# The second sequence's mLSTM cell moved ahead of all attention, four heads to a step

## The chip, the cores and the metric

The kernel runs on one core of one Trainium2 chip. The metric is device time in microseconds of one launch. A core has five engines that each work through their own queue: TensorE (PE, matrix products; PEld is its weight loads), VectorE (DVE), ScalarE (ACT), GpSimd (POOL) and SyncE (SP, which only issues transfers). Transfers are also issued by ACT and POOL. Lines such as L421 are lines of the kernel before.

## The reference, cut to what matters

Eight sequences of 512 tokens and 256 features go through four stages, each added to the running value:

```
x = x + tanh(g_xattn[0]) * mlstm_cell(layernorm(x), ctx, ctx)   # 8 heads of 32
x = x + tanh(g_ffn[0])   * attention32_and_experts(layernorm(x))  # 32 heads of 8, then 8 experts
x = x + tanh(g_xattn[1]) * cross_attention(ctx, layernorm(x))   # 16 heads of 16
x = x + tanh(g_ffn[1])   * product_key_memory(layernorm(x))     # 4096 rows
```

The change concerns the first stage alone. For each head the cell computes

```
log_f = log_sigmoid(fg);  cs = cumsum(log_f)
log_D = cs[:, None] - cs[None, :] + ig[None, :]     # lower triangle, else -inf
D     = exp(log_D - max(log_D))
C     = (q @ k.T) / sqrt(32) * D
h     = (C / (max(|sum(C)|, exp(-max)) + eps)) @ v
```

and then normalises h over the features. Here q is the normalised x, and k and v are the context.

## The kernel before, in words

**Stages.** `attention_phase` does the first three stages of all eight sequences (m = 0 to 7). The memory (the fourth stage) follows and isn't touched.

**What sets the order.** Inside `attention_phase` the order of TensorE's instructions is the order in which Python emits them. All other engines are ordered by a scheduler that weighs the whole program. The emitting loop goes through 24 attention jobs of 16 steps: ("A", m, f), half f of the 32 heads, and ("C", m, 0), the cross attention. A step has a first pass for one job, which finds the maxima (`maxima`: scores at L421, then the row maximum on DVE at L439), and a second pass for an earlier job (`exponentials`: scores at L421 again, exp on ACT at L468; then `values`, L484). Both go in two half steps. At the start there are steps in which nothing of attention is ready, then 19 steps with a first pass alone, and from then on mostly both.

Beside the steps, `beside` fills TensorE's queue from eight *lanes*, generators that are asked in order of priority. A lane yields a cost (it has emitted that much TensorE work), ("wait", t) (come back later by the plan's clock), ("rest", key) (come back when the key is in `rested`), or ("take", flag) for the one PSUM bank that cells and experts share. The lanes are: `between` (loads each job's operands into SBUF and marks it ready), `values1`, `after`, `before` for sequences 0, 2, 3, ... 7 with the class `Tiles`, `behind` (experts and the cross attention's queries), `before` for sequence 1 with the class `Lent`, `contexts` (the cross attention's keys and values), and `fill` (first-layer products of the memory, the filler).

**A cell.** `before` calls `cell(m, own, loaded)` and then `queries(m, own, Xa)`, which makes q, k and v of the 32 heads and stores them to DRAM. In `cell`: layer norm of x (statistics L98, normalise L107), transposes to features (L350), the gates (`gp`, L736), a chain on ACT and DVE for the running sums and maxima (L745 to L774), the maxima out to DRAM (`nM_d`, L776) and back to all partitions. Then per pair of heads and per block c of 128 keys: a triangular mask on POOL, the decay exp on ACT, scores on PE, their product with the decay on DVE, and sums on PE. `close` transposes the sums (L804) and divides.

There are two forms of that middle part. `all_pairs`, used for sequence 0 alone, has eight steps of two pairs (four heads) each; it reads all four maxima tiles at once, into the `qa`/`ka` tiles of set 1 that attention doesn't use yet (L644), keeps decays in set 2 and in attention's `pr` tiles, and scores in attention's `sc` banks and sums in its `av` bank. It is emitted in one piece. Sequences 1 to 7 use the loop over pairs, which has one maxima tile (two for `Lent`) and small banks of its own, and yields after each block (L829 fetch, L847 mask, L855 decay, L877 scores, L882 product, L862 sums).

`Lent` holds the second cell's tiles in places of the expert weights, which are free at the start. Its x and context are loaded by SP (L579, L622, L582), those of other sequences by POOL behind `settled`, the last piece of sequence 0's v. `Tiles.begin` of the third sequence also spreads its context into `cte` on POOL (L227).

Of the kernel before, what the change touches and what calls it, by code (L numbers as in the profile page):

```python
# [21 lines left out]
P = 128  # L22
# [14 lines left out]
def kernel(  # L37
# [27 lines left out]
    nc = tc.nc  # L65
# [114 lines left out]
    def attention_phase(ctx: ExitStack):  # L180
# [86 lines left out]
        for w, src in ((wo2, w0[3]), (wq3, w3[0])):  # L267
# [20 lines left out]
        sets = [  # L288
            tuple(cst.tile([P, 4, S], F32, name=f"{name}{i}") for name in ("qa", "ka"))
            for i in range(3)  # L290
        ]
# [270 lines left out]
        class Tiles:  # L562
# [23 lines left out]
            def context(self, m):  # L586
                return load_context(m, "cTc"), cte

            ahead = False

            def maximum(self, n=0):
                return cel.tile([P, 2, S], F32, name="mb", bufs=1)

            def pair(self):
# [8 lines left out]
        class Lent(Tiles):  # L603
# [18 lines left out]
                self.loader.dma_start(cT, cxT[order[m]].rearrange("(k p) s -> p k s", p=P))  # L622
                return cT, self.cte

            ahead = True

            def maximum(self, n=0):
                return self.more[:, n % 2].rearrange("p c d -> p (c d)").rearrange(
                    "p (i s) -> p i s", i=2
                )  # L630

            def pair(self):
                self.n += 1
# [2 lines left out]
            def stream(self):  # L636
                return self.more[:, 1]

        def all_pairs(qT, cT, ce, nM_d, aT, close):


            room = [t[:, 2 * i : 2 * i + 2] for t in sets[1] for i in range(2)]
            for pair in range(4):
                nc.sync.dma_start(  # L644
                    room[pair], nM_d[2 * pair : 2 * pair + 2].partition_broadcast(P)
                )
            spare = [t[:, 2 * i : 2 * i + 2] for t in sets[2] for i in range(2)]
            pds, avs = {}, {}
            steps = [(g, c) for g in range(2) for c in range(NC)]

            def decay(n):
                g, c = steps[n]
                s0 = c * P
                for pair in (2 * g, 2 * g + 1):
                    mb = room[pair]

                    nc.gpsimd.affine_select(
                        out=mb[:, :, s0 : s0 + P], in_=mb[:, :, s0 : s0 + P],
                        pattern=[[0, 2], [1, P]], compare_op=ALU.is_ge,
                        fill=NEG, base=0, channel_multiplier=-1,  # L660
                    )
                    pd = pds[pair, c] = (
                        spare[c - 1 + pair % 2] if c % 2
                        else prb.tile([P, 2, S], F32, name="pr", tag="pr")
                    )
                    for i in range(2):
                        h = 2 * pair + i
                        nc.scalar.activation(
                            pd[:, i, s0:], mb[:, i, s0:], AF.Exp, bias=aT[:, c, h : h + 1]
                        )  # L670

            def weigh(n):
                g, c = steps[n]
                s0 = c * P
                two = {
                    pair: ps_sc.tile([P, 2, S], F32, name="sc", tag="sc")
                    for pair in (2 * g, 2 * g + 1)
                }
                for pair, sc in two.items():
                    for i in range(2):  # L680
                        r = 32 * (2 * (pair % 2) + i)
                        nc.tensor.matmul(
                            sc[:, i, s0:], cT[r : r + 32, g, s0 : s0 + P], qT[r : r + 32, g, s0:],
                            start=True, stop=True,
                        )
                for pair, sc in two.items():
                    pd = pds[pair, c]
                    nc.vector.scalar_tensor_tensor(
                        pd[:, :, s0:], sc[:, :, s0:], 1.0 / math.sqrt(32.0), pd[:, :, s0:],
                        ALU.mult, ALU.mult,  # L690
                    )

            def sums(n):
                g, c = steps[n]
                for pair in (2 * g, 2 * g + 1):
                    if c == 0:
                        avs[pair] = (
                            ps_av.tile([P, S], F32, name="av", tag="av") if pair % 2
                            else ps_ac.tile([P, S], F32, name="cav", tag="ac")
                        )  # L700
                    for i in range(2):
                        h = 2 * pair + i
                        nc.tensor.matmul(
                            avs[pair][64 * i : 64 * i + 64, c * P :],
                            ce[:, c, 33 * h : 33 * h + 64],
                            pds[pair, c][:, i, c * P :], start=(c == 0), stop=(c == NC - 1),
                        )

            decay(0)
            decay(1)  # L710
            for n in range(len(steps) + 1):
                if n < len(steps):
                    weigh(n)
                if n > 0:
                    sums(n - 1)
                    g, c = steps[n - 1]
                    if c == NC - 1:
                        for pair in (2 * g, 2 * g + 1):
                            close(pair, avs[pair])
                if n + 2 < len(steps):  # L720
                    decay(n + 2)

        def cell(m, own, loaded):
            b = order[m]
            qn, cT, ce = loaded or own.begin(m)
            yield ("wait", 4)
            yield from layernorm(qn, qn, "q" + own.user)
            qT = own.features("qT")
# [46 lines left out]
            nM_d = drm.tile([8, S], F32, name="nM_d")  # L775
# [9 lines left out]
            aT = small.tile([P, NC, 8], F32, name="aT")  # L785
# [9 lines left out]
            def store_sums(av):  # L795
                avs = trp.tile([P, S], F32, name="avs", tag="pk", bufs=2)
                nc.any.tensor_copy(avs, av)
                return avs
# [21 lines left out]
                    ALU.mult,  # L820
                )

            if m == 0:
                all_pairs(qT, cT, ce, nM_d, aT, lambda pair, av: close(pair, store_sums(av)))
            mbs = {}

            def fetch_maximum(pair):
                mbs[pair] = own.maximum(pair)
                nc.sync.dma_start(  # L829
                    mbs[pair], nM_d[2 * pair : 2 * pair + 2].partition_broadcast(P)  # L830
                )

            for pair in range(4) if m else ():

                if pair not in mbs:
                    fetch_maximum(pair)
                    yield ("wait", 2.5)
                mb = mbs[pair]
                if own.ahead and pair < 3:
                    fetch_maximum(pair + 1)  # L840
                g = pair // 2
                pds = {}

# [27 lines left out]
                av = own.bank("cav")  # L871
# [24 lines left out]
                yield ("wait", 1.0)  # L896
                close(pair, avs)
                yield 0.7
                if pair == 2:
                    rested.add(("cell", m))  # L900
            Xa = own.stream()
            with behind_first():
                nc.gpsimd.dma_start(Xa, x[b].rearrange("(c p) d -> p c d", p=P))
# [87 lines left out]
        def begin(m):  # L991
            for f in range(2):
                i, last = block2_set(m, f)
                yield ("rest", ("q", m))
                if last is None and i:
                    prepare(i)
                if last:
                    yield ("rest", last)
                for half, src, name in zip(sets[i], qks[m], "qk"):
                    yield ("rest", (name, m))  # L1000
                    spread(half, src, 32 * f, 8)
                    if name == "q":
                        blank(half)
                yield ("wait", LANDING)
                ready.add(("A", m, f))
                yield ("rest", ("v_d", m))
                yield ("rest", ("A", m - 1, f))
                nc.sync.dma_start(v0[f][:, :, : 16 * 9], vds[m][:, f])
                ready.add(("v0", m, f))
# [271 lines left out]
        ready, rested = set(), set()  # L1281

        def before(sequences, tiles):
            own, loaded = tiles(), None
            if tiles is Lent:
                loaded = own.begin(sequences[0])
                yield ("rest", ("k", 0))
            for m in sequences:
                if m == 2:
                    yield ("rest", ("cell", 1))  # L1290
                Xa = yield from cell(m, own, loaded)
                yield from queries(m, own, Xa)
            if tiles is Lent:
                rested.add(("lent", 0))
                load_first(0)
                load_second(0)
# [239 lines left out]
    def close(p, h):  # L1536

        nc.tensor.matmul(
            scores[p, h], ones3, crow[:, 512 * h : 512 * h + 512], start=False, stop=True
        )  # L1540
# [115 lines left out]
    pieces = activations()  # L1656
# [192 lines left out]
    ahead = weights_of(*steps[0])  # L1849
# [3 lines left out]
    for g, (p, u) in enumerate(steps):  # L1853
        n, step = g // 8, g % 8
        q = p + 2
        cf, ahead = ahead, weights_of(*steps[g + 1]) if g + 1 < len(steps) else None
# [100 lines left out]
```

## Time and profile before

| | us |
|---|---|
| median of 3 runs | 3799.53 (3795.38 to 3808.29) |
| the profiled execution | 3788.9 |
| its span | 3787.1 |
| first attention score (L421) | 100.86 |
| first step with both passes | 234 |
| PE busy in the span | 3495.5 (92%) |

In the profile each engine has a busy time; a row of the timeline gives the start, the time that a group of instructions took, the engine, line and operation, what it wrote and read, and in brackets the idle time of that engine before it and what ended it. A windows row gives the stretch, its length, the busy time of the engines in the order PE, PEld, DVE, ACT, POOL with the number of instructions, the granted TensorE clock, the DMA share and GB/s.

### The profile page before, as it was taken

The numbers are of one execution on the slowest core, as the hardware profiler recorded it, in microseconds if no ns is written. First come the engines' busy times: TensorE is split into PE (matmuls) and PEld (weight loads), VectorE is DVE, ScalarE is ACT, GpSimd is POOL, SyncE is SP. The second block draws the span as 40 slices with busy tenths as digits, with TensorE's granted clock in tenths as the row PEclk, the third lists the DMA queues.
The fourth block names the chain that finished last, engine by engine and source line by source line (L and its number), as shares of the span: only waits on it lengthen the run. The fifth ranks groups of instructions, "written<-read, shape, count | busy, mean of one in ns | idle before, by whom it ended". The sixth has DMA issues, their size and how long they took to land.

```text
span 3787.1 us, 76231 instructions
## 1 busy us (share of the span) xinstructions
PE 3495.5 (92%) x31049; PEld 1827.5 (48%) x31049; DVE 2244.9 (59%) x5490; ACT 1755.2 (46%) x2300; POOL 601.5 (16%) x646
## 2 busy tenths in 40 slices
PE   5789888998999999999999999999899999999998
PEld 2333333443443444344433444434346777777776
DVE  4565655665555555555555553544422789999993
ACT  2135444453444445444555444444442455555551
POOL 3121102111100110101100110100000133333331
PEclk7789999999999999999999999999999999999999
DMA  3422212322412332323231232320434433333331
GB/s 112 127 83 82 69 44 71 92 75 65 125 51 78 92 90 77 94 82 98 83 90 57 92 102 81 104 88 23 146 119 144 127 116 106 105 105 106 107 106 38
DMA packets 225195, 345.35 MB, mean 91 GB/s; under 512 B 25982, under 2 KB 173470, under 8 KB 216542
## 3 DMA queue, kind: packets, MB, share of 16 engines
q1 hardware_dynamic: 206796, 277.43, 24.5%
q0 software_dynamic: 16864, 62.46, 5.6%
q8 instruction: 244, 4.00, 0.4%
q14 instruction: 107, 0.88, 0.1%
q10 hardware_dynamic: 1184, 0.58, 0.1%
HBM read 238.50 MB, written 101.09 MB: 90 GB/s over the span
## 4 chain that ended last, share of the span: by engine, by line
PE 66%; DVE 7%; ACT 2%; DMA 1%; issue 1%; SPq 0%; DVEq 0%; ACTq 0%
PE sc L421 16%; PE acc L1799 12%; PE ps_hd L131 11%; PE av L484 6%; DVE nm L439 5%; PE cf L1779 4%; PE ps_sim L1531 3%; PE ps_y L1063 2%; PE ps_h L1044 2%; PE ps_q L380 2%; PE ps_p L369 1%; PE ps_hl L131 1%; PE cav L862 1%; PE csc L877 1%; PE ps_g L1180 1%
## 5 line engine op out<-in xcount | busy, mean ns | idle before, releaser
L439 DVE TENSOR_REDUCE nm<-sc 128x2 f32<-128x1024 f32 x768 | 939.0, 1225 | 926.2 <-PE sc L421 924.2
L468 ACT ACTIVATE pr<-sc 128x1024 f32<-128x1024 f32 x768 | 782.8, 1023 | 928.9 <-PE sc L421 928.4
L421 PE MATMUL sc<-ka,qa 32*128 32x512 f32 x3072 | 906.2, 652 | 96.9 <-DVE nm L439 96.0
L421 PE MATMUL sc<-qa,ka 32*128 32x512 f32 x3072 | 858.3, 647 | 29.1 <-ACT pr L468 27.3
L1799 PE MATMUL acc<-up_sb,gs 64*128 64x256 f32 x4096 | 467.9, 381 | 1.3 <-DVE gs L1788 1.3
L421 PEld LDWEIGHTS sc<-ka,qa 32*128 32x128 f32 x3072 | 246.3, 186 | 437.4 <-DVE nm L439 248.6
L131 PE MATMUL ps_hd<-xT,dw 128*64 128x256 f32 x3584 | 431.2, 385 | 20.7 <-DMA dw<-in_down 9.5
L484 PE MATMUL av<-pr,v 128*32 128x512 f32 x3072 | 414.3, 611 | 3.0 <-DMA v<-v_d 2.9
L1799 PEld LDWEIGHTS acc<-up_sb,gs 64*128 64x128 f32 x4096 | 389.6, 187 | 52.4 <-issue 4.9
L131 PEld LDWEIGHTS ps_hd<-xT,dw 128*64 128x64 f32 x3584 | 244.7, 137 | 236.2 <-issue 107.5
L1769 POOL TENSOR_TENSOR m<-o,cwT 128x1024 f32<-128x1024 bf16 x128 | 243.6, 1903 | 580.5 <-DVE o L1767 240.3
L1246 ACT COPY hb<-ps_hd 128x512 f32<-128x512 f32 x224 | 131.0, 585 | 301.3 <-PE ps_hd L131 264.6
L421 PEld LDWEIGHTS sc<-qa,ka 32*128 32x128 f32 x3072 | 232.4, 184 | 67.7 <-ACT pr L468 55.7
L484 PEld LDWEIGHTS av<-pr,v 128*32 128x32 f32 x3072 | 60.8, 108 | 296.0 <-issue 291.9
L855 ACT ACTIVATE pd<-mb,aT 128x512 f32<-128x512 f32 (+1 forms) x224 | 113.6, 554 | 159.8 <-PE cav L862 98.2
L1788 DVE TENSOR_TENSOR gs<-cf,gs 128x1024 f32<-128x1024 f32 x128 | 155.7, 1218 | 42.7 <-PE cf L1779 27.3
L1779 PEld LDWEIGHTS cf<-m,m 64*64 64x64 f32 x8192 | 134.8, 135 | 38.7 <-issue 38.3
L1779 PE MATMUL cf<-m,m 64*64 64x64 f32 x8192 | 152.4, 222 | 0.8 <-DVE gs L1788 0.7
L1765 ACT CAST m<-o 128x1024 f32<-128x1024 bf16 x128 | 133.7, 1045 | 39.5 <-DVE o L1763 35.7
L847 POOL TENSOR_SCALAR_AFFINE_SELECT mb<-mb 128x256 f32<-128x256 f32 x112 | 45.3, 406 | 640.9 <-ACT pd L855 382.4
L1044 PE MATMUL ps_h<-fT,w1e 128*128 128x256 f32 x512 | 135.3, 400 | 5.7 <-DVE o L512 3.3
L1063 PE MATMUL ps_y<-w2e,heT 128*128 128x256 f32 x512 | 133.1, 400 | 4.1 <-issue 1.9
(264 smaller groups left out, 4020.0 us busy)
## 6 DMA issues: line engine op xcount, KB each, us to landing
h_d<-hb SPq DMA_DIRECT2D x224, 256.0 KB
gs<-h_d SPq DMA_DIRECT2D x56, 1024.0 KB
dw<-in_down SPq DMA_DIRECT2D x112, 256.0 KB
w1e<-in_w POOLq DMA_DIRECT2D x16, 1024.0 KB, 5.5
w2e<-in_w POOLq DMA_DIRECT2D x16, 1024.0 KB, 6.6
mb<-nM_d SPq DMA_DIRECT2D x28, 512.0 KB
cT<-in_cxT POOLq DMA_DIRECT2D x22, 512.0 KB, 4.5
qk_d<-pk SPq DMA_DIRECT2D x32, 256.0 KB
```

The source lines that it names most:

```text
L131: nc.tensor.matmul(ps[64 * q : 64 * q + 64, :], dw[:, k, :], runs[:, :, q, :], start=(k == 0), stop=(k == NK - 1),)
L421: nc.tensor.matmul(sc[:, i, :], lhs[r : r + 32, g, c * P : (c + 1) * P], rhs[r : r + 32, g, :], start=True, stop=True,)
L439: newest = nc.vector.tensor_reduce(self.nm[:, c, 2 * half : 2 * half + 2, g], sc, AX.X, ALU.max, negate=True)
L468: nc.scalar.activation(mine[jj], sc, AF.Exp)
L484: nc.tensor.matmul(self.av[32 * j : 32 * j + 32, :], self.va[:, c, h * (self.hd + 1) : h * (self.hd + 1) + 32], pr[j // 2][:, j % 2, :], s ...
L1044: nc.tensor.matmul(ps[:, :D], w1e[:, k, f * P : (f + 1) * P], fT[:, k, i * D : (i + 1) * D], start=(k == 0), stop=(k == NK - 1),)
L1063: nc.tensor.matmul(py[:, c, :], hT[:, f, c * P : (c + 1) * P], w2e[:, f, :], start=(f == 0), stop=(f == NF - 1),)
L1765: nc.scalar.copy(m1, o1)
L1769: nc.gpsimd.tensor_tensor(m2, o2, tokens(cw), ALU.mult)
L1779: nc.tensor.matmul(cf[64 * q : 64 * q + 64, h, s, :], m2[rows, 4 * q + s // 2, :, s % 2], m1[rows, 4 * q + s // 2, :, s % 2], start=True, ...
L1788: nc.vector.tensor_tensor(gv, cf.rearrange("p h s i -> p i h s"), gv, ALU.mult)
L1799: nc.tensor.matmul(accs[n][q], gs[n % 2][rows, i, :], up_sb[rows, i, :], start=(i == 0), stop=(i == 63),)
```

## The change

The second sequence's cell uses `all_pairs` too. Its four maxima tiles lie in the places lent to it (two in `more`, two in `pds`, which held its maxima and its decays). `all_pairs` becomes a generator: for sequence 0 it is still emitted in one piece, for sequence 1 it yields 1.6 after every step. The wait of the second cell for sequence 0's keys is gone, so it starts at once. The first attention job is marked ready only when that cell is done. The prefetch of maxima that `Lent` had in the loop is gone.

```diff
@@ Tiles
-            ahead = False
-            def maximum(self, n=0):
+            def rooms(self):
+                return [t[:, 2 * i : 2 * i + 2] for t in sets[1] for i in range(2)]
+            def maximum(self):
                 return cel.tile([P, 2, S], F32, name="mb", bufs=1)
@@ Lent
-            ahead = True
-            def maximum(self, n=0):
-                return self.more[:, n % 2].rearrange("p c d -> p (c d)").rearrange(
-                    "p (i s) -> p i s", i=2
-                )
+            def rooms(self):
+                both = self.more.rearrange("p n c d -> p n (c d)").rearrange(
+                    "p n (i s) -> p n i s", i=2
+                )
+                return [both[:, 0], both[:, 1], self.pds[:, 0], self.pds[:, 1]]
+            def maximum(self):
+                return self.rooms()[0]
@@ all_pairs
-        def all_pairs(qT, cT, ce, nM_d, aT, close):
-            room = [t[:, 2 * i : 2 * i + 2] for t in sets[1] for i in range(2)]
+        def all_pairs(room, qT, cT, ce, nM_d, aT, close):
...
                 if n + 2 < len(steps):
                     decay(n + 2)
+                yield 1.6
@@ cell
-            if m == 0:
-                all_pairs(qT, cT, ce, nM_d, aT, lambda pair, av: close(pair, store_sums(av)))
-            mbs = {}
-            def fetch_maximum(pair):
...
-            for pair in range(4) if m else ():
-                if pair not in mbs:
-                    fetch_maximum(pair)
-                    yield ("wait", 2.5)
-                mb = mbs[pair]
-                if own.ahead and pair < 3:
-                    fetch_maximum(pair + 1)
+            if m < 2:
+                pieces = all_pairs(
+                    own.rooms(), qT, cT, ce, nM_d, aT,
+                    lambda pair, av: close(pair, store_sums(av)),
+                )
+                for cost in pieces:
+                    if m:
+                        yield cost
+                rested.add(("cell", m))
+            for pair in range(4) if m > 1 else ():
+                mb = own.maximum()
+                nc.sync.dma_start(mb, nM_d[2 * pair : 2 * pair + 2].partition_broadcast(P))
+                yield ("wait", 2.5)
...
-                if pair == 2:
-                    rested.add(("cell", m))
@@ begin (lane between)
                 yield ("wait", LANDING)
+                if m == 0:
+                    yield ("rest", ("cell", 1))
                 ready.add(("A", m, f))
@@ before
                 loaded = own.begin(sequences[0])
-                yield ("rest", ("k", 0))
```

More of the change, by code (lines that the diff above doesn't have):

```diff
@@ L821, in close @@
                 )
-            if m == 0:
-                all_pairs(qT, cT, ce, nM_d, aT, lambda pair, av: close(pair, store_sums(av)))
-            mbs = {}
-            def fetch_maximum(pair):
-                mbs[pair] = own.maximum(pair)
-                nc.sync.dma_start(
-                    mbs[pair], nM_d[2 * pair : 2 * pair + 2].partition_broadcast(P)
-                )
-            for pair in range(4) if m else ():
-                if pair not in mbs:
-                    fetch_maximum(pair)
-                    yield ("wait", 2.5)
-                mb = mbs[pair]
-                if own.ahead and pair < 3:
-                    fetch_maximum(pair + 1)
+            if m < 2:
+                pieces = all_pairs(
+                    own.rooms(), qT, cT, ce, nM_d, aT,
+                    lambda pair, av: close(pair, store_sums(av)),
+                )
+                for cost in pieces:
[6 more added lines that the diff above has]
+                yield ("wait", 2.5)
                 g = pair // 2
```

## The prediction

> **What bounds the kernel now.** I read the page first: its slices, then its chain.
>
> ```profile
> span 3787.1 us, 76231 instructions
> PE   5789888998999999999999999999899999999998
> PE 66%; DVE 7%; ACT 2%; DMA 1%; issue 1%; SPq 0%; DVEq 0%; ACTq 0%
> ```
>
> PE is at nine tenths from the fourth slice on and carries the chain; only the first 300 us are loose. So I cut those into stretches (columns as explained above):
>
> ```profile
> 0.00:24.00 24.00, 8.75 (x21) 3.41 (x21) 8.99 (x29) 6.92 (x11) 11.45 (x19) 0.99 0.64 170
> 24.00:56.00 32.00, 17.32 (x88) 7.37 (x88) 15.16 (x21) 16.87 (x35) 12.34 (x20) 0.61 0.35 123
> 56.00:101.00 45.00, 24.20 (x126) 15.35 (x124) 19.03 (x57) 2.84 (x7) 9.28 (x12) 0.77 0.25 66
> 101.00:142.00 41.00, 27.61 (x96) 12.93 (x96) 22.38 (x33) 6.10 (x10) 10.00 (x17) 0.78 0.66 167
> 142.00:234.00 92.00, 76.62 (x310) 34.64 (x312) 58.53 (x90) 17.22 (x34) 12.27 (x29) 0.82 0.27 86
> 300.00:2600.00 2300.00, 2145.83 (x14123) 928.92 (x14122) 1254.53 (x1882) 1086.14 (x1326) 266.99 (x378) 0.99 0.28 81
> ```
>
> Until 101 us PE works half the time: the start is one chain of latencies, not work. The timeline of the start has its posts:
>
> ```profile
> 9.63 2.73 DVE L107 TENSOR_SCALAR qn<-qn,ln_mv,ln_rs 128x256 f32<-128x256 f32 x4 [1.97 <-POOL ln_rs L104]
> 11.59 0.37 SPq L579 DMA_DIRECT2D qn<-in_x  x1
> 13.67 3.49 PE L736 MATMUL gp<-qT,gwm 128*40 128x512 f32 x4
> 78.10 2.21 PE L350 MATMUL ps_t<-ident,xn 128*128 128x128 f32 x8 [12.60 <-DVE xn L938]
> 98.86 2.08 PE L380 MATMUL ps_q<-ws,nT 128*128 128x256 f32 x4 [7.07 <-ACT vk L972]
> 100.86 1.78 PE L421 MATMUL sc<-ka,qa 32*128 32x512 f32 x8
> ```
>
> Attention's first score stands right behind the first sequence's v. Later, PE's waits between 300 and 2600 us are mostly attention's own:
>
> ```profile
> PE sc L421 <- DVE nm L439: 76.5, 145, 2.2
> PE sc L421 <- ACT pr L468: 23.1, 13, 5.3
> ```
>
> A half step can't take less than its scores (1.07) and the maximum on them (1.22), 2.47 us in bare steps; other PE work of up to 1.4 us hides in it.
>
> **What the Trainium skill says.** "PSUM — Partial Sum Buffer" (Engine vs sequencer instructions): ACT's, DVE's and POOL's queues are strict FIFO and matmuls start in program order. The trace agrees: the 98.86 product and all behind it waited 7.07 us. So order within a queue is what counts here. "ScalarE: Activation LUTs" (What ACT_TABLE_LOAD costs) has about 1283 ns for a load; the trace has 1.28 us. "TensorE: Matmul & The Clock Gate" (HAM oscillation) says that idle gaps slow the clock again; the granted clock of 0.61 to 0.82 here agrees.
>
> **The change, part by part.** I compared the order of both programs, engine by engine. The number of attention steps and their pairing is the same (19 alone at first, 359 double). What moves is what stands ahead.
>
> *(1) DVE waits for the second sequence's x: +12.1.* In DVE's new order the second sequence's four L98 and four L102 stand between the first sequence's L102 and its L107. They wait for the transfer issued at 11.59. On its queue 2.8 MB are due up to and with it (0.25 + 0.05 + 0.5 + 0.5 + 4 x 0.25 + 0.5), and the queue moved 2.95 MB in the first 20 us:
>
> ```profile
> q1 hardware_dynamic: 3652, 2.95, 51.9%
> ```
>
> So it lands just short of 20; I take 19.7. Statistics 1.5 and aggregates 0.4 follow: L107 starts at 21.7 instead of 9.63. Everything of the first sequence is queued behind it.
>
> *(2) +3.9 to the first sequence's running sums.* Two of the second sequence's L107 stand between, and wait for POOL (1.97 after the aggregates, then 2 x 0.68): +2.0. Four more transposes precede the first gates on PE (+0.8), and a copy of 0.58 with its wait precedes the Ln table (+1.1). The chain that was at 23.2 (Ln) is at about 39, +16.
>
> *(3) +2.3 to the first weighing.* The second cell's gate chain is ahead of the first L688 on DVE: L745 (1.5) after the first chain's end (29.5 + 16 = 45.4), three ACT steps of 0.63 with two table loads of 1.28 (to 50.9), then 5.4 on DVE (0.68 + 1.21 + 0.68 + 1.21 + 0.92 + 0.72): 56.3, where 37.97 + 16 = 54 was due. The ACT loads alone hide under the maxima's landing (36.2 + 16). Sum so far +18.3.
>
> *(4) Eight steps of the second cell: +23.* The first cell's eight steps took 37.97 to 63.56, 3.2 each. In PE's new order four stand before the transposes of xn (+12.3 by walking through: 4 x 3.2, and half a step's sums and `close` more, less what fits into POOL's 2.6 ahead of xn), and the rest behind the first sequence's last v, with two more transposes (about 11: three steps of 2.8 and 2.5 for the copies and `close`). The work of the first sequence's v doesn't overlap with these, since L380 stands in front. First score: 100.9 + 18.3 + 23.3 = 142. **+41**.
>
> *(5) DMAs and queues.* The second cell's four maxima (0.5 MB each) were spread over 150 to 230 us; now two go out after its chain, two when its transposes (L781) free the places, at about 85. On SP these two wait with the first sequence's x, zero rows, memory weights and q behind them; x is due at about 92, so it isn't late. On POOL its 16 masks go ahead of the first sequence's rsqrt, and I find them done by 92.5, just in time: nothing, up to 3 us if not.
>
> *(6) What comes back: the third sequence's loads, -9.* They are released by the last v:
>
> ```profile
> 108.85 0.85 POOL L582 DMA_DIRECT2D Xa<-in_cx  x1
> 116.90 1.16 POOL L227 COPY cte<-Xa 128x512 f32<-128x512 f32 x2 [6.40 <-DMA Xa<-in_cx]
> ```
>
> The copy stands ahead of the next rsqrt on POOL, and PE idled 3.3 + 3.4 + 2.9 us for it at 107 to 124. In the new order the last v lies some 5 us ahead of the first score instead of behind it, so these 9 go.
>
> *(7) One pair of table loads, -4.7.* The third cell's Ln fell among attention's exps (PE waited at 264, a step of 10.5 instead of 5.8 us); now it comes before the first exp.
>
> ```profile
> 264.80 1.28 ACT L468 ACT_TABLE_LOAD   x1
> ```
>
> *(8) PE work that left the steps: -7.* The cell's work later would take 35.7 us on PE (L877 14.8, L862 12.2, gates 4.1, transposes 4.6, by means between 300 and 2400 us). But the work beside the first-pass-only steps stays equal (50 us; the third sequence and q, k, v move up), and beside the double steps 27 us go. I added this gap by gap in PE's order and took for each half step the larger of 2.47 and 1.07 plus its gap: 2333 us before, 2326 after. Only 7 of 27 come back, because 18 more half steps fall bare and the rest sink to the floor, most at the end, where the filler runs out for five steps. (The trace has 2443 for these steps: 110 are other waits.)
>
> Sum: +41 - 9 - 4.7 - 6.8 = +20.5. By PE's idle time: the start +7, bare half steps +20.6, less 13.7, makes +14; the two differ by how a slow clock counts the cell at the start. I take **+16**: 3788.9 becomes 3805, and as the median lies 10.6 above the profiled execution, the median becomes 3815.5. A measurement of this kernel can tell about 0.3%, 11.4 us.
>
> **The rivals.**
> *All of the moved work returns* (not slower): every freed PE microsecond shortens the steps, 35.7 + 13.7 = 49 against 41: -8, 3791. For: PE is at 93% of its time from 300 us on. Against: the bare half steps. It decides where more than (41 - 13.7) / 35.7 = 76% returns; I have 19% by (8). Chance 0.15, about half of it beyond 0.3%.
> *The start overlaps better*: the second cell's steps fit into idle PE between the first sequence's chain, so that (4) costs 11 and not 23: first score near 130, +4, 3803. For: half of PE is idle. Against: FIFO order on PE and DVE. Chance 0.2.
> *Nothing returns*: new waits (DVE copies for q, k, v with two `pk` places, masks behind transfers) eat (6) to (8): +38, 3838. Chance 0.15.
> *The change doesn't do what it says*: the program has 48 instead of 56 scores of each size at L877 and 16 instead of 8 at L682; I give it nothing.
>
> **How the numbers follow.** The likeliest (+16, its own range +6 to +28) has 0.5. Slower by over 0.3%: 0.36 of that, 0.15 of the third rival, 0.06 of the second, with some for a worse start, together 0.6. Faster: 0.07 of the first rival, 0.03 each from the other two, 0.12. Same: 0.28. The range goes from -12 (first rival with the clock's gain of 3 at a later start) to +42: 3788 to 3842.
>
> **What would show it.** First L107 at 21 to 22 us (1); first L736 at 28; first L688 near 56; L350 on xn near 103; first L421 at 138 to 146; the idle time of PE behind it small (6); no Ln load among exps before 300 us; double steps of 5 us in the last 400 us of attention; span up by 10 to 25. The prediction is wrong if the first score is before 130, or if the double steps' total falls by over 20 us.

## The result, and the profile after

The changed kernel takes 3812.05 us (median of 20 runs, 3799.06 to 3818.66) where the kernel before takes 3796.71 (20 runs beside it): a ratio of 1.0032, 95% interval 1.0023 to 1.0041, or +12 us (the two medians differ by 15). The forecast was +16 as the likeliest, slower with 0.6. The profiled execution has 3809.98 us, 2 under the median.

The page's slices and the shares of its chain, then the stretches that the prediction showed of before (length; busy time and instructions of PE, PEld, DVE, ACT, POOL; granted clock; DMA share; GB/s):

```profile
span 3808.2 us, 76216 instructions
...
PE   4778899898999989999999999989899999999998
...
PE 44%; DVE 4%; DMA 1%; ACT 1%; issue 0%; SPq 0%; DVEq 0%; ACTq 0%
```

```profile
0.00:24.00 24.00, 1.93 (x7) 1.36 (x8) 7.98 (x32) 1.79 (x3) 11.89 (x20) 1.00 0.75 208
24.00:56.00 32.00, 16.40 (x56) 5.98 (x54) 17.16 (x26) 17.60 (x28) 6.41 (x12) 0.80 0.31 99
56.00:101.00 45.00, 32.11 (x216) 13.80 (x216) 31.12 (x76) 24.22 (x53) 17.43 (x32) 0.84 0.20 68
101.00:142.00 41.00, 27.21 (x135) 16.82 (x132) 15.76 (x42) 5.66 (x16) 9.67 (x16) 0.83 0.45 136
142.00:234.00 92.00, 72.87 (x304) 39.42 (x304) 60.71 (x88) 16.12 (x31) 34.46 (x46) 0.85 0.52 154
300.00:2600.00 2300.00, 2131.89 (x13980) 910.90 (x13977) 1243.26 (x1839) 1075.16 (x1299) 258.95 (x360) 0.98 0.28 80
```

The chain's shares sum to 50% here and to 77% before, so the view didn't follow the whole of it, and I don't read the two against each other. (In the changed kernel the same statements lie a few lines further down: L740 is L736 of before, L691 is L688.) In the first 24 us PE has hardly begun (1.93 us busy, 8.75 before). From 56 to 101 it does 216 products instead of 126, and still between 300 and 2600 us it is busy for 14 us less than before, at a clock one hundredth lower. The posts of the start, from the timeline:

```profile
10.29 0.47 SPq L579 DMA_DIRECT2D qn<-in_x  x1
18.19 1.41 DVE L98 BATCH_NORM_STATS2 ln_st<-qn 128x6 f32<-128x256 f32 x4 [10.48 <-DMA qn<-in_x]
19.79 0.70 DVE L107 TENSOR_SCALAR qn<-qn,ln_mv,ln_rs 128x256 f32<-128x256 f32 x2
21.44 2.34 DVE L107 TENSOR_SCALAR qn<-qn,ln_mv,ln_rs 128x256 f32<-128x256 f32 x6 [0.95 <-POOL ln_rs L104]
25.38 3.64 PE L740 MATMUL gp<-qT,gwm 128*40 128x512 f32 x4
52.46 2.33 DVE L691 SCALAR_TENSOR_TENSOR pr<-sc,pr 128x1024 f32<-128x1024 f32 x2
98.55 1.09 PE L350 MATMUL ps_t<-ident,xn 128*128 128x128 f32 x8
124.06 2.07 PE L380 MATMUL ps_q<-ws,nT 128*128 128x256 f32 x4 [5.48 <-ACT vk L971]
137.32 1.14 PE L421 MATMUL sc<-ka,qa 32*128 32x512 f32 x8
...
133.96 0.85 POOL L582 DMA_DIRECT2D Xa<-in_cx  x1
141.19 1.16 POOL L227 COPY cte<-Xa 128x512 f32<-128x512 f32 x2 [3.86 <-DMA Xa<-in_cx]
```

DVE stands idle for 10.48 us, for the second sequence's x, with the first sequence's L107 queued behind (the two pieces at 19.79 are its own; the six from 21.44 on are its other two and the second sequence's four). The first weighing (product of scores and decays, L691) is at 52.5 instead of 38.0, the first score at 137.3 instead of 100.9. The third sequence's loads (two last lines) now go out 3.4 us ahead of the first score, not 8 us behind it. And PE's waits between 300 and 2600 us:

```profile
PE sc L421 <- DVE nm L439: 93.1, 160, 1.8
PE sc L421 <- ACT pr L468: 15.4, 11, 2.6
```

Before, the first was 76.5 us. My reading is that with less other work PE arrives sooner at the next score and waits for the maximum.

Both kernels were profiled a second time (e11, e12), which shows what belongs to the program: these waits come again to within 1 to 3 us (76.4 and 94.2), but the two executions of before differ by 17 us and those of after by 9. That is nearly all in half-clock time: stretches in which the granted TensorE clock is 0.5, here 3.4 us long or multiples of it. Over the 20 runs of the changed kernel, too, time follows the granted clock (correlation -0.87; 0.975 at 3799.06, 0.97 at 3818.66). So the stages are compared by the mean of two executions:

| us, mean of two | before | after | difference |
|---|---|---|---|
| start to first score | 101.6 | 137.0 | +35.4 |
| first score to first exponential (first pass alone) | 134.6 | 122.3 | -12.3 |
| first exponential to end of attention | 2623.2 | 2607.4 | -15.8 |
| of it: PE at work, put at full clock | 2400.4 | 2365.4 | -35.0 |
| of it: PE idle | 180.0 | 193.3 | +13.3 |
| of it: lost to half clock (half the length of the stretches that begin there) | 42.6 | 48.6 | +6.0 |
| the memory behind it | 936.5 | 937.1 | +0.7 |

The differences sum to +8, against +12 by the ratio of 20 runs each. (Idle time is what no matmul of the trace covers.) The third part in one line: 35 us of PE work left the double steps, and 19 of them came back as gaps and as a slow clock. The gaps repeat (180 and 180 before, 192 and 195 after); the 6 us of half clock don't stand out of the scatter (36 and 49 before, 53 and 44 after). Over whole runs the changed kernel's clock isn't the slower one: its mean is 0.972 in 20 runs, and that of before is 0.971 in the 43 beside e1 to e4.

### The profile page after: what moved, and what is told of

Read it like the earlier page. It is cut to its first block, busy times and chain, and to the rows that moved or that the text cites. A ratio compares the mean times of both kernels' runs of the same rounds, so it can differ in the third digit from the quotient of the medians.

```text
span 3808.2 us, 76216 instructions
## 1 busy us (share of the span) xinstructions
PE 3493.5 (92%) x31049; PEld 1822.3 (48%) x31049; DVE 2243.9 (59%) x5468; ACT 1757.5 (46%) x2307; POOL 603.6 (16%) x646
## 4 chain that ended last, share of the span: by engine, by line
PE 44%; DVE 4%; DMA 1%; ACT 1%; issue 0%; SPq 0%; DVEq 0%; ACTq 0%
PE acc L1800 12%; PE sc L421 8%; PE ps_hd L131 7%; PE cf L1780 4%; PE ps_sim L1532 3%; PE av L484 3%; DVE nm L439 3%; PE ps_y L1065 1%; PE ps_h L1046 1%; PE ps_hl L131 1%; PE ps_q L380 1%; PE ps_p L369 1%; PE ps_sim L1539 1%; PE ps_g L1182 0%; PE tr L1631 0%; PE ot L505 0%
## 5 line engine op out<-in xcount | busy, mean ns | idle before, releaser
L421 PE MATMUL sc<-qa,ka 32*128 32x512 f32 x3072 | 868.0, 654 | 18.4 <-ACT pr L468 16.3
L484 PE MATMUL av<-pr,v 128*32 128x512 f32 x3072 | 422.6, 623 | 3.0 <-DMA v<-v_d 2.9
L131 PEld LDWEIGHTS ps_hd<-xT,dw 128*64 128x64 f32 x3584 | 245.6, 138 | 228.3 <-issue 102.2
L856 ACT ACTIVATE pd<-mb,aT 128x512 f32<-128x512 f32 (+1 forms) x192 | 97.4, 553 | 104.3 <-PE cav L863 61.4
```

Source lines behind the costliest of these rows:

```text
L131: nc.tensor.matmul(ps[64 * q : 64 * q + 64, :], dw[:, k, :], runs[:, :, q, :], start=(k == 0), stop=(k == NK - 1),)
L421: nc.tensor.matmul(sc[:, i, :], lhs[r : r + 32, g, c * P : (c + 1) * P], rhs[r : r + 32, g, :], start=True, stop=True,)
L484: nc.tensor.matmul(self.av[32 * j : 32 * j + 32, :], self.va[:, c, h * (self.hd + 1) : h * (self.hd + 1) + 32], pr[j // 2][:, j % 2, :], s ...
```

## The experiments

The last three columns (us) are each from one profiled execution, except for before and after. That execution can lie some way off its run's median: 13.5 us above it in e6, 10 and 13 below it in e9 and e10, within 6 in the others. So differences of under some 10 us in the last column say little.

| run | ratio to before | first score | first exponential | from there to the end of attention |
|---|---|---|---|---|
| before (two profiles) | 1 | 100.9, 102.2 | 234, 238 | 2618, 2628 |
| after (two profiles) | 1.0032 | 137.3, 136.6 | 260, 259 | 2611, 2604 |
| e1 before, second cell's middle left out | 1.0016 (1.0008 to 1.0024) | 103.1 | 242 | 2625 |
| e2 after, its eight steps left out | 1.0045 (1.0031 to 1.0058) | 123.3 | 252 | 2628 |
| e3 after, layer norm behind the first cell's | 1.0053 (1.0040 to 1.0067) | 142.2 | 264 | 2611 |
| e4 before, third loads earlier | 0.9979 (0.9970 to 0.9989) | 101.9 | 227 | 2621 |
| e5 e1 with PE's part put back | 1.0065 (1.0049 to 1.0081) | 103.6 | 220 | 2668 |
| e6 before, idle products at the start | 1.0020 (1.0008 to 1.0032) | 100.6 | 236 | 2643 |
| e7 e3, attention doesn't wait | 1.0030 (1.0021 to 1.0039) | 124.5 | 258 | 2623 |
| e8 before, attention waits for the cell | 1.0163 (1.0147 to 1.0179) | 175.5 | 306 | 2626 |
| e9 four-head form in the old place | 1.0089 (1.0072 to 1.0107) | 96.8 | 242 | 2644 |
| e10 e9 and e4 | 1.0085 (1.0068 to 1.0103) | 99.1 | 240 | 2643 |

**What is late PE work worth? (e1, e5)**

```diff
-            for pair in range(4) if m else ():
+            if m == 1:
+                nc.gpsimd.memset(hk, 1.0)
+                rested.add(("cell", m))
+            for pair in range(4) if m > 1 else ():
```

> The kernel before without the second sequence's decay exponentials, scores, sums and closing (its hk is filled with ones instead, so its output differs); everything else, its loads, gates and projections, stays. It shows what 30 us of PE work are worth that late in attention. Prediction's step 8 (a fifth of it returns): 5 to 9 us faster than before, ratio 0.998. Rival 'all of the moved work returns': 30 to 36 us faster, ratio 0.991. 'Nothing returns': ratio 1.000. First score unchanged near 101 us in all three.

Measured: 6 us slower. The work is gone (36 us less of it on PE behind the first exponential) and nothing comes back. PE's waits between 260 and 2600 us, of before and then of e1:

```profile
PE sc L421 <- DVE nm L439: 78.7, 151, 2.2
```

```profile
PE sc L421 <- DVE nm L439: 110.4, 180, 5.2
```

The waits for the maxima grow by 32 us. Behind the first exponential PE is idle for 201 us in all instead of 180, and 60 us are lost to half clock instead of 36 and 49; the granted clock is lower in the runs too, 0.967 in the mean of 22 against 0.971 in 43 of before. "All of the moved work returns" falls: -30 to -36 was expected, +6 came. e5 keeps the cell's scores and sums on PE in e1's program, without the other engines' part:

```diff
+            for pair in range(4) if m == 1 else ():
+                g = pair // 2
...
+                        nc.tensor.matmul(
+                            sc[i][:, s0:], cT[r : r + 32, g, s0 : s0 + P], qT[r : r + 32, g, s0:],
+                            start=True, stop=True,
+                        )
...
+                            qT[:, 0, s0:], start=(c == 0), stop=(c == NC - 1),
```

> As e1, but the second cell's scores and sums stay on PE (on q's features instead of the decayed scores; nothing reads them), without its masks, exponentials, products and closing. Some 27 us more of PE work than e1. Theory 'PE's gaps lower the clock': the gaps that e1 left are filled, the half-clock time before 250 us goes back from 58 x 2 to about 51 x 2 us or less, and the time is at or below the kernel before and below e1: 3790 to 3799 us. Rival 'late PE work is paid like other work and e1 was slower for another reason (the order of the other engines)': 3806 us or more, up to 3830.

Measured: 3827, on the rival's side; filling PE didn't restore the time. The theory's first sign did come (96 us of half clock ahead of the first exponential instead of e1's 116), but its time didn't. Its waits for maxima are short again (77.3 us in the same stretch), yet PE is idle for 200 us in all, as in e1, and its granted clock is lower (0.966 over the run): 73 us lost to half clock after the first exponential against 36 and 49 in before. So gaps and clock are where the time goes, but how much of it can't be read from the amount of PE work alone. That the place of the work in the order decides is a guess which no run here tests; why e1 and e5 have more gaps and half clock than before stays open.

**The parts of the start (e2, e3, e7).** e2 leaves the eight steps out of the changed kernel, with the same three lines as e1 in front of `all_pairs`.

> The changed kernel without the second sequence's eight all_pairs steps (its hk is filled with ones, so its output differs). Late work as in e1, the queue order at the start as after. Steps 1 to 3 (the wait for the second x and what follows it) should stand alone: first score near 117 to 120 us instead of 101, and the time 12 to 18 us above e1. If the start's delay is from the eight steps alone, the first score is near 103 and the time equals e1.

First score 123.3, 20 above e1; time 11 us above e1. So steps 1 to 3 of the prediction alone delay the first score by 20 (put at 18), and the eight steps add only 14 to that. e3 takes step 1 away:

```diff
-            nc.vector.bn_stats(st[:, c, :], src[:, c, :])
+            with tc.issue_after(normal[3]) if user == "q2" and len(normal) == 4 else nullcontext():
+                nc.vector.bn_stats(st[:, c, :], src[:, c, :])
...
+                yield ("rest", ("ln", 0))
```

> The changed kernel, but the second cell's layer norm is held behind the first cell's L107 (statistics too), so that DVE doesn't wait for the second x there. First L107 back at 9.6 us, first weighing near 38 us. All eight steps of the second cell then stand behind the first sequence's last v on PE: first score 125 to 132 us instead of 137. Prediction's steps 1 to 3: the time falls by as much as the first score, 5 to 12 us below after (ratio to before 1.000 to 1.002). If the wait for x is hidden anyway (PE waits for other things), no change: 1.003.

First L107 at 10.2 as wanted, first weighing at 43.4 (the second cell's statistics now wait for x ahead of the first gates), and the first score comes at 142.2, later than in after; both cases of the expectation miss, in the score and in the time. The timeline of e3 on PE:

```profile
86.35 0.45 PE L355 MATMUL ps_t<-ident,xn 128*128 128x128 f32 x1 [11.35 <-DVE xn L943]
...
113.48 2.09 PE L690 MATMUL sc<-qT,cT 32*128 32x512 f32 x8
...
142.22 1.14 PE L426 MATMUL sc<-ka,qa 32*128 32x512 f32 x8
```

With the second cell started later, all of its eight steps (113 to 142) lie behind the first sequence's v, and the 11 us gap ahead of xn, which four of them filled in after (98.55 there, without a gap), is open again. The delays of the two cells are not a sum: the wait for x costs 9 us at the first weighing, and the overlap that it allows gives them back and 5 more. In e7 the same program lets attention start without the second cell; only the first values wait:

```diff
-                if m == 0:
-
-                    yield ("rest", ("cell", 1))
                 ready.add(("A", m, f))
...
+                if m == 0:
+                    yield ("rest", ("cell", 1))
                 nc.sync.dma_start(v0[f][:, :, : 16 * 9], vds[m][:, f])
```

> As e3, and attention's first pass doesn't wait for the second cell any more: the wait stands ahead of the first values only, so that the eight all_pairs steps lie between the first-pass-only steps, where PE has gaps. Theory 'the price is attention's late start': first score near 105 to 112, first exponential 235 to 245 us, time 3785 to 3800. If the eight steps cost their full PE time wherever they stand: first exponential near 260 and time as e3, 3815 or more.

First score 124.5, first exponential 258, 3813: near the second case. The first score is 13 us earlier than in after and the first exponential at the same time, so an earlier first score alone brought nothing. An earlier first exponential isn't enough either: it comes at 220 in e5 and at 242 in e9, which are 25 and 34 us slower than before.

**Place and form (e8, e9, e10).** e8 adds the changed kernel's wait to before, so that three of the cell's four pairs go ahead, pair by pair (the second cell's statistics held behind the first L107, as in e3):

> The kernel before, where attention waits for three of the second cell's four pairs (the changed kernel's wait) but the cell goes pair by pair as before. The place of the cell without its four-head form. First score 150 to 175 us instead of 137; by the price of a late start (0.4 us per us, as in after: +12 for +36) 20 to 30 us above before; if every microsecond of start is paid, 45 us or more above; if the four-head form saves nothing, as after, 3812.

First score 175.5, 62 us slower, of 74 us of delay: the expectation's case in which the start is paid (45 or more). That is 39 us more than in after at the first score and 50 us more in the time, but the form isn't the only difference: e8 keeps before's wait for the first sequence's keys, so its second cell makes its gates at 109 us, behind the first sequence's v, and after makes them at 34. From its first scores of pairs (124.5) to the first attention score e8 takes 51 us for the three pairs; e3's eight steps take 29 us for all four (113.5 to 142.2). So some 22 of the 39 us lie in the form. e9 is the opposite: the four-head form where the cell was before, with e7's wait, e3's held statistics and

```diff
             if tiles is Lent:
                 loaded = own.begin(sequences[0])
+                yield ("rest", ("k", 0))
```

> The changed kernel's four-head form of the second cell in the old place: the cell starts when the first sequence's k is out, as before, attention's first pass starts without it, and only the first values wait for it, so that the eight steps stand between first-pass-only steps. First score back at 101 us. If the price of the change is its place (all that delays the first score) and the form itself is cheap: first exponential 234 to 245 us, time 3785 to 3800. If the eight steps cost their 30 us of PE wherever they stand: first exponential near 260, time 3810 or more.

3834, 34 us slower, although the first exponential is at 242. In the profiled execution, itself 27 us slower than the mean of before's two, most of the loss is behind it: 2644 us to the end of attention, of them PE idle 195 (180 before) and half clock 56. The forecast for this run failed on both theories. The double steps hardly got lighter: the trace has 8 us less PE work there than in before, where after has 35 less. Counting products by tile says where the work went: after has 32 sums and 32 scores of the third sequence's pairs ahead of the first exponential, e9 has none (384 of each behind it, after 352), and 24 more products for q, k and v lie behind it too. What left the double steps was replaced by the next cell. Why its gaps also grew is open. e10 adds e4's edit to it:

> e9 with e4's edit (third sequence's loads released by the first v piece). If the two add: 6 to 9 us below e9. If the waits of these loads are now covered by the eight steps: equal to e9 within 3 us.

Equal to e9: its second case. That the eight steps cover these waits isn't shown.

**The third sequence's loads (e4).**

```diff
-                if m == 0:
+                if m == 0 and c == 0:
                     settled = last
```

> The kernel before, with one edit: the third sequence's loads (behind 'settled') are released by the first of the first sequence's four v pieces and not by the last. Step 6: PE's idle time between 107 and 124 us shrinks by up to 9 us, second first-pass step starts near 112 to 115 instead of 122, and the time falls by 6 to 9 us (ratio 0.998). If the gain is used up by other waits of the first-pass-only steps, ratio 1.000.

8 us faster by the ratio. The same stretch of before and of e4:

```profile
101.00:125.00 24.00, 13.01 (x44) 6.73 (x44) 11.43 (x20) 1.06 (x4) 9.28 (x16) 0.71 0.71 166
```

```profile
101.00:125.00 24.00, 21.37 (x67) 9.12 (x65) 14.49 (x23) 1.65 (x5) 6.54 (x13) 0.70 0.74 171
```

PE does 8.4 us more in it at the same clock. It is the one version here that beats before.

**Does the slow clock at the start matter? (e6)**

```diff
+        def warm(n, src):
+            keep = ps_m.tile([P, S], F32, name="keep", tag="m")
+            for _ in range(n):
+                nc.tensor.matmul(keep, ident, src, start=True, stop=True)
```

> The kernel before with 40 idle products (identity x q's features, 128x512, into a PSUM bank that nobody reads) in three gaps of the first cell: 14 ahead of the transposes of the running sums, 10 behind the first weighing's scores, 16 ahead of the transposes of xn. Theory 'clock': the half-clock stretch from 23.7 to 47.6 us and those at 54 and 68 us go, first score from 101 to 92 to 97 us, time 4 to 9 us lower (3790 to 3795). Rival 'the start is a chain of latencies, the clock doesn't matter there': first score 101 or later by what the products get in the way, time equal or higher (3799 to 3810).

The clock does as expected (0.974 in the mean of 14 runs, 0.971 in 35 of before), but the time doesn't; e6's rows:

```profile
24.00:56.00 32.00, 29.49 (x139) 12.78 (x139) 14.76 (x26) 15.82 (x35) 11.23 (x20) 1.00 0.34 124
...
93.00:101.00 8.00, 2.45 (x8) 1.62 (x12) 0.00 (x0) 0.53 (x2) 0.83 (x2) 0.55 0.36 91
```

Full clock to 93 us, first score 100.6 as in before (100.9 and 102.2): the products that run faster wait for the next transfer or copy all the same. The start is a chain of latencies. Where its 0.2% of loss arise stays open: the profiled execution has 2643 us behind the first exponential, but it is 13.5 us slower than the median of e6.

**Program or chance? (e11, e12)**

> The kernel before once more, for its half-clock stretches between 300 and 2860 us. If they belong to the program: most of the 15 stretches of the first profile come again within 10 us of their place. If they are chance: their places differ, and their sum (24 us of lost time in the first profile) moves by 10 us or more.

> The changed kernel once more, for the run of six half-clock stretches between 384 and 463 us. If it belongs to the program, it comes again, and steps 40 to 60 of attention take about 147 us again where the kernel before takes 121 us; if it is chance, they take 122 to 130 us.

Both in part. In before, stretches at 266, 491, 515, 577, 597, 860, 1116, 1222, 1478 and 2321 us come again (within 14 us of their places, most of them later with the later start), others are new; their loss goes from 36 to 49 us. (Between 300 and 2860 us alone there are 13 and 18 stretches with 31 and 44 us of loss; the expectation's 15 stretches count from the first exponential on, and its 24 us don't come out of the trace.) In after, those at 408 and 425 come again and those at 435 and 456 don't; steps 40 to 60 take 140 us instead of 147, against 122 before, so most of that stretch's excess is work that lies there (716 products instead of 672, some 13 us of PE at full clock); the rest is half clock (15 and 7 us for 2 and 3).

## Why the prediction was right, step by step

- **(1), (2), (3)** The wait of DVE: right, and the x landed at 18.2 instead of 19.7, so the first L107 starts at 19.8 instead of 21.7. The first weighing is at 52.5 instead of 56.3: +14.5 for +18.3; the gates came at 25.4 and not 28. (The terms of (3) as written, 45.4 + 1.5 + 3 x 0.63 + 2 x 1.28, make 51.4 and not 50.9.)
- **(4)** From there to the first score +22 (84.9 for 62.9), for +23. As a size right, as a sum not. The transposes of xn came at 98.6 and not at 103, so +6 us lie ahead of them for the +12.3 of the four steps there, and +16 behind them for the 11 of the rest: two misses that cancel. And e2 and e3 show that the terms of (1) to (4) overlap (20 without the eight steps, 14 more with them; 41 with step 1 taken away). So it is in part luck that the first score, 137.3 and 136.6, lies just under the 138 to 146 of the forecast.
- **(5)** Right; POOL's masks didn't hold the first sequence's rsqrt (82.4 and 88.9; the one ahead of it waits for DVE), and the maxima sent at 79.4 didn't hold its x.
- **(6)** -9 was put on the first-pass-only steps; they became 12.3 us shorter. In e4, which makes this one edit, they are 9.5 us shorter (125.1 for 134.6), and the run gains 8. Right.
- **(7)** Right in place: the third cell's Ln is loaded at 168 us, ahead of the first exponential. The first eleven double steps are 9 us shorter instead of 4.7, and a half-clock stretch of 6.8 us at 266 (270 in the second profile) went with the stall.
- **(8)** -7 was right as a sum, not as a distribution. By numbered steps of attention, mean of two executions, after less before: 30 to 40, -2; 40 to 60, +21; 60 to 80, -21; 80 to 160, +3; 160 to 240, +13; 240 to 320, -3; 320 to 360, -19; behind them +2: in all -6. Each of these repeats within 4 us, but for 7 us at 40 to 60. So it is the program that does it, and not where I put it: the end, where the filler was to run dry, got 19 us shorter, and the middle longer. Part of the 19 is another matter: a wait of 7.8 us for the load of `dw` at 2316 in before (7.4 the second time) is missing in after. Without it the sum would be about +1, so that it agrees with -7 is luck. "Only 7 of 27 come back" has support from e1, where nothing comes back, but isn't settled: e1, e2, e3, e8 and after have the cell's work out of the double steps and take 2604 to 2628 us there, mean 2619, against 2618 and 2628 of before, a gain of 4 with a scatter of 10 (after's two profiles alone have 16 less than before's two).

So the sum, 41 - 9 - 5 - 7 = 20, and +14 by idle time, stood for 35 - 12 - 9 - 6 = 8 by two profiles and 12 by the ratio. The order and the signs of the terms are what the prediction got right; the start was put 6 us too high and what comes back 7 too low. Both errors point the same way. Neither of the two signs of being wrong came (the first score isn't before 130, and the double steps fell by 16 us, not by over 20). But inside (4) and (8) the close agreement is by chance. Half clock behind the start is no term of the sum; what the traces show of it there (+6) is within the scatter.

Of the rivals, "the start overlaps better" has some truth: of the eight steps, put at 23 us, only 14 show at the first score. "Nothing returns" was wrong for (6) and (7). "All returns" is excluded by e1, and by the changed kernel itself: 35 us of PE work left its double steps, and they became 16 us shorter.

## What to carry to other kernels

PE's busy share, 93% between 300 and 2600 us here, does not say that PE work is worth its time: leave the work out and look (e1 became slower). Work taken out of the steps left gaps behind (e1: waits for DVE's maxima 110 us for 79), and work put ahead of them cost 62 us of 74 in e8, and 12 of 35 in the changed kernel, where other stages gave some back. Where a sum of terms agrees with the result, look at the terms: here two of them agreed by errors that cancelled. The gain that was there was one release: loads held behind the last of four pieces, where the first of them would do (e4, 8 us for one condition).

## What the runs showed of the hardware

- Half clock comes after a thin stretch, not only after a long gap. The Trainium skill, "TensorE: Matmul & The Clock Gate" (HAM oscillation — how this bites in real kernels), gives as a rule to have no idle gaps of PE over some 3.4 us. In both profiles of after, PE has no gap over 3.4 us between 300 and 2860 us (the longest are 3.2 and 3.3), yet there are 23 and 18 half-clock stretches; in the 3.4 us ahead of a stretch PE was 11 to 86% busy, mostly 40 to 70%. Cut into windows of 3.41 us from the edges of the stretches, the full-clock time of both profiles shows how far this goes:

  | PE busy in the window | windows | with half clock right behind |
  |---|---|---|
  | under 50% | 20 | 18 |
  | 50 to 60% | 33 | 14 |
  | 60 to 70% | 61 | 4 |
  | 70 to 90% | 207 | 5 |
  | 90% and more | 1122 | 0 |

- They often follow a change of ACT's table: 19 of these 41 begin within 7 us of the start of a table load, where such time is 14% of that from 300 to 2860 us. Most changes have none behind them, though: 15 of 82 do. In after:

```profile
405.07 1.28 ACT L761 ACT_TABLE_LOAD   x1
407.01 1.28 ACT L468 ACT_TABLE_LOAD   x1
```

  PE waited 2.58 us for the exponential behind it, and 10.2 us at half clock began at 408.1 (at 404.9, after loads at 402 and 403, in the second profile). The 1.28 us of a load agree with the Trainium skill, "ScalarE: Activation LUTs" (What ACT_TABLE_LOAD costs), which has about 1283 ns. If the half clock is put down to the two loads, they cost more than their 2 x 1.28 us; no run here takes them away.
- Two executions of one program differ by 17 us (before) and by 9 (after), nearly all of it half-clock time, while its waits repeat within 3 us. A difference of 0.3% needs many runs; the first pair of profiles gave +21 and the second -5, where 20 runs each gave +12.
